# Edge loads moved to the head of two queues, the relation table's making moved behind the edge words, and the copy of the input moved behind the first pass

## The chip, the cores and the metric

The kernel runs on one core of a Trainium2 chip. A core has five engines that run their own instruction streams: TensorE (PE; its weight loads are listed as PEld), VectorE (DVE), ScalarE (ACT), GpSimd (POOL) and SyncE (SP). Transfers between the memory on the device (DRAM here) and the core's on-chip memory are DMAs. In this kernel SP and ACT issue the plain ones and POOL the indirect ones (gathers); each engine issues its DMAs in the order of its stream, and 16 DMA engines carry them out. The metric is the device time of the program in microseconds, the median of several runs.

## The reference

Four layers are applied one after the other to x (3125 nodes x 256), each with a residual: x + layer(layernorm(x)).

- A graph layer with three rounds over 103,125 directed edges (sorted by destination). Each round takes the mean of h over the incoming edges of every node, then a linear layer, a normalization with given mean and variance, and a relu.
- A mixture of 16 experts, the top 2 for each node.
- A second graph layer, in which every edge has one of 500 relation types.
- A mixture of 8 experts, the top 2 for each node.

The parts that matter here, cut down:

```python
edge_index = jnp.stack([src, dst])
x = x + _L0_gnn_ref(_layernorm(x), edge_index, ...)     # three rounds
x = x + _L0_ffn_ref(_layernorm(x)[None], ...)[0]
x = x + _L1_gnn_ref(_layernorm(x), edge_index, edge_type_500, relation_emb, ...)
x = x + _L1_ffn_ref(_layernorm(x)[None], ...)[0]

# in _L1_gnn_ref, for every edge:
gate = sigmoid(r_uv.reshape(E, -1) @ gate_w.T + gate_b)  # depends on the relation alone
m = clifford_linear(h_src * r_uv, msg_w, msg_b) * gate
```

## The kernel before, in words

Nodes are padded to 25 blocks of 128 (`NB`, `P`). The edges are laid out as 806 columns of 128 (`ET`). The kernel is written in a tile framework: the text gives operations and tiles, and the framework chooses the order in which instructions stand on each engine and places the semaphore waits. An engine runs its own stream strictly in that order, so a waiting instruction holds up everything behind it on the same engine.

**Relation table** (lines 263 to 280). The 500 relation vectors are loaded (`rel`), each is multiplied by the gate weights and summed (`prod`, `dot`), the sigmoid of the sum is the gate, and the gated vector with its gate is stored to DRAM as `r_rows`. VectorE does the products and sums, ACT the sigmoids, SP the loads and the store.

**Prologue** (391 to 470). The edge ends and types are loaded (`ids`, line 399), x into `h` (401), and on ACT's queue the weights `ww` (404, 405) and the five norm vectors (410). `first_i` (416) is the first destination of each column; from it VectorE and TensorE count where each half block of 64 destinations begins, and `begin` (433) holds 50 window starts. From the edge ends VectorE makes six words for each edge (`word`, 437 to 450), which SP stores to DRAM as `edge_words` (451). The norm vectors are folded into the weights (454 to 464), x is layer-normalized in place (466), and row 0 is replaced by the mask row (467).

**First pass** (641 to 665), which is round 1 of the first graph layer together with the sorting of the edges. For each destination block `load` reads two window starts from `begin` into registers of SP (512) and loads the two windows of 20 columns of edge words (513, `win`); `rank` begins with `kb` (523); `permute`, `lay` and `build` turn the window into a 128 x 3200 count matrix, `cell`, which is stored to DRAM as `cells` (632) for the two later rounds; `sums_of` multiplies it with the three parts of h that `spread` (339 to 353: `hT`, `part_hi`, `rest`, `part_lo`, `own`) made for each source block; `finish` writes h. `done` is the last tile that `finish` returned.

**Relation gathers** (289 to 312). The second graph layer needs `r_rows` in the order of the edge slots. All through the first pass and later stages, `fetch_relations` has POOL gather 3 x 128 rows of `r_rows` into `rel_rows` (301), and SP stores them to DRAM as `r_seq` (312) when they have landed. VectorE's operation `paced` (297) ties each group to a point of the other work. There are 4 landing buffers. `r_rows` is first read by the first gather.

**Boundary.** After the first pass a number, `loops`, tells whether a slow path must run (684). It is 0 for these inputs; the loop at 694 is skipped, but all engines meet there. Then come rounds 2 and 3 (`spread_later`, line 853, and `sums_of` with cells loaded by SP, 841). In round 2 VectorE also sums each cell over its rows (`some_src`, 863).

**Copy of x.** `base` in DRAM (320) holds a copy of the input. The third round's `finish` reads it block by block (384) for the residual. In the kernel before it is made by one DMA from DRAM to DRAM on SP (660).

Of the kernel before, what the change touches and what calls it, by code (L numbers as in the profile page):

```python
# [49 lines left out]
P = 128  # L50
# [4 lines left out]
ET = 806  # L55
D = 256
KD = D // P
NREL = 500
# [16 lines left out]
def bcast(ap, n):  # L75

    return bass.AP(tensor=ap.tensor, offset=ap.offset, ap=[[0, P], [1, n]])
# [3 lines left out]
def gnn_moe_kernel(  # L81
# [9 lines left out]
    nc = tc.nc  # L91
# [165 lines left out]
    W = D + 1  # L257
# [2 lines left out]
    of_group = [range(t, min(t + RG, NM)) for t in range(0, NM, RG)]  # L260
    r_rows = dram.tile([NREL, W], F32, name="r_rows")
    r_seq = [dram.tile([P, len(g) * W], F32, name=f"r_seq{i}") for i, g in enumerate(of_group)]
    with tc.tile_pool(name="rel_pre", bufs=1) as pre:
        gw_sb = pre.tile([P, D], F32, name="gate_w")
        nc.sync.dma_start(gw_sb, bcast(g1_gw, D))
        gb_sb = pre.tile([P, 1], F32, name="gate_b")
        nc.sync.dma_start(gb_sb, bcast(g1_gb, 1))
        NR = NREL // 4
        rel = pre.tile([NR, 4, W], F32, name="rel")
        nc.sync.dma_start(rel[:, :, :D], g1_rel.rearrange("(g p) d -> p g d", p=NR))  # L270
        for g in range(4):
            prod = pre.tile([NR, 4, 64], F32, name="prod", bufs=2)
            dot = pre.tile([NR, 1], F32, name="dot", bufs=2)
            nc.vector.tensor_mul(prod, rel[:, g, :D].rearrange("p (k c) -> p k c", k=4),
                                 gw_sb[:NR, :].rearrange("p (c k) -> p k c", k=4))
            nc.vector.tensor_reduce(dot, prod, AX.XY, ALU.add)
            nc.scalar.activation(rel[:, g, D:W], dot, AF.Sigmoid, bias=gb_sb[:NR, :])
            nc.vector.tensor_scalar(rel[:, g, :D], rel[:, g, :D], rel[:, g, D:W], None,
                                    op0=ALU.mult)
        nc.sync.dma_start(r_rows.rearrange("(g p) d -> p g d", p=NR), rel)  # L280


    next_r = iter(range(len(of_group)))
    rel_ctx = ctx.enter_context(ExitStack())
    paced = rel_ctx.enter_context(tc.tile_pool(name="paced", bufs=1)).tile([P, NM], I32, name="paced")
# [3 lines left out]
    def fetch_relations(n, after):  # L289

        for i in islice(next_r, n):
            g = of_group[i]
            rows = stage.tile([P, RG, W], F32, name="rel_rows")
            types = paced[:, g[0]:g[-1] + 1]
            nc.vector.scalar_tensor_tensor(
                types, after[:, :len(g)], 0, main_t[:, g[0]:g[-1] + 1],
                op0=ALU.bitwise_and, op1=ALU.bitwise_or)
            for j, t in enumerate(g):  # L300
                nc.gpsimd.indirect_dma_start(  # L301
                    out=rows[:, j, :], out_offset=None, in_=r_rows,
                    in_offset=bass.IndirectOffsetOnAxis(ap=types[:, j:j + 1], axis=0))
            store_relations()
            landing.append((i, rows))
# [14 lines left out]
    base = dram.tile([NP, D], F32, name="base")  # L320
    acc_d = dram.tile([NB, P, W], F32, name="acc_d")
    h = xs
    with ExitStack() as block:
# [66 lines left out]
        with ExitStack() as first:  # L390
            one = first.enter_context(tc.tile_pool(name="g0_one", bufs=1))
            begin = one.tile([1, 2 * NB], I32, name="begin")
            with ExitStack() as prep:
                pre = prep.enter_context(tc.tile_pool(name="g0_pre", bufs=1))
                psum = prep.enter_context(tc.tile_pool(name="g0_preps", bufs=2, space=PSUM))
                ids = []
                for ap in (src, dst, etype):
                    ids.append(pre.tile([P, ET], I32, name="ids", bufs=2))
                    nc.sync.dma_start(ids[-1], ap)
                for b0 in range(0, NB, 5):  # L400
                    nc.sync.dma_start(
                        h[:, b0:b0 + 5, :],
# [4 lines left out]
                for name, ap in (("b", g0_b), ("gamma", g0_gamma), ("beta", g0_beta),  # L407
# [3 lines left out]

                TF = 13
                first_i = pre.tile([ET // TF, TF], I32, name="first_i")
                nc.sync.dma_start(first_i, dst[0:1, :].rearrange("o (p k) -> (o p) k", k=TF))
                first_f = pre.tile([ET // TF, TF], F32, name="first_f")
                nc.vector.tensor_copy(first_f, first_i)
                nodes = pre.tile([ET // TF, 2 * NB, TF], F32, name="nodes")
                nc.gpsimd.iota(nodes, pattern=[[P // 2, 2 * NB], [0, TF]], base=0,  # L420
                               channel_multiplier=0, allow_small_or_imprecise_dtypes=True)
                nc.vector.tensor_tensor(
                    nodes, first_f[:, None, :].to_broadcast([ET // TF, 2 * NB, TF]), nodes,
                    op=ALU.is_lt)
# [24 lines left out]
                nc.vector.tensor_scalar(cap, cap, 1.0, None, op0=ALU.add)  # L449
                nc.vector.tensor_copy(et, ids[2])  # L450
                nc.sync.dma_start(words, word)


                nc.scalar.activation(bn["rvar"], bn["rvar"], AF.Sqrt, bias=eps)
# [6 lines left out]
                for half in range(2):  # L461
                    for k in range(KD):
# [6 lines left out]
                                                        ap=[[D, 1], [1, D]]))  # L469
# [172 lines left out]
            for i in range(NB + 3):  # L642
                if i < NB:
                    loaded[i] = load(i)
                    ranked[i] = rank(i, loaded[i])
                if 0 <= i - 1 < NB:
                    moved[i - 1] = permute(i - 1, loaded.pop(i - 1), *ranked.pop(i - 1))
                    lay(i - 1, moved[i - 1])
                    if i > 1:
                        fetch_relations(1, words_of(moved[i - 1]))  # L650
                if 0 <= i - 2 < NB:
                    if i > 2:
                        fetch_relations(1, words_of(moved[i - 2]))
                    built[i - 2] = build(i - 2, moved.pop(i - 2))
                for b in range(i * SB, min((i + 1) * SB, NB)):
                    spread(b, 0, psum.tile([P, D + 1], F32, name="z", bufs=2)[:, :D],
                           psum.tile([P, 4, P], F32, name="block", bufs=2).rearrange(
                               "p a q -> p (a q)"))
                if i == 3:
                    nc.sync.dma_start(base, x)  # L660
                if 0 <= i - 3 < NB:
                    z = sums_of(i - 3, built.pop(i - 3), 0, psum)
                    done = finish(i - 3, z, 0)
                    if i > 3:
                        fetch_relations(1, done.bitcast(I32))

        with ExitStack() as flags:
            one = flags.enter_context(tc.tile_pool(name="g0_deg0", bufs=1))
# [16 lines left out]
        with ExitStack() as slow:  # L685
# [8 lines left out]
            with tc.For_i(0, n_slow, 1):  # L694
# [4 lines left out]
                                                        ap=[[D, 1], [1, D]]))  # L699
# [10 lines left out]
                with tc.For_i(0, ET, 1) as i:  # L710
                    for e in range(2):
                        oh = []
                        for part, n in zip(ends[e], (NB, P)):
                            c = slow_work.tile([P, 1], F32, name="end_column", bufs=4)
# [3 lines left out]
                                                    op0=ALU.is_equal)  # L718
# [8 lines left out]
                for layer in range(3):  # L727
# [4 lines left out]
                    for b in range(NB):  # L732
                        mean = slow_work.tile([P, D], F32, name="mean")
                        nc.vector.tensor_scalar(mean, acc[:, b, :], inv_dst[:, b:b + 1], None,
                                                op0=ALU.mult)
# [18 lines left out]
        with ExitStack() as later:  # L754
# [104 lines left out]
            for b, cell in enumerate(ahead_of(load_cell, 2)):  # L859
                z = sums_of(b, cell, 1, psum,  # L860
                            {12: lambda: fetch_relations(1, places(b, psum))})
                d = work.tile([P, NB], F32, name="some_src")
                nc.vector.tensor_reduce(d, cell, AX.X, ALU.add)  # L863
                nc.vector.tensor_add(deg, deg, d)
                done = finish(b, z, 1)
# [25 lines left out]
            for b, cell in enumerate(ahead_of(load_cell, 2)):  # L891
# [4 lines left out]
                done = finish(b, z, 2)  # L896
# [351 lines left out]
    with ExitStack() as block:  # L1248
# [14 lines left out]
        with ExitStack() as prep:  # L1263
            pre = prep.enter_context(tc.tile_pool(name="g1_pre", bufs=1))
# [5 lines left out]
            for kern, w, name in ((km, g1_mwt, "mw"), (ku, g1_uwt, "uw")):  # L1270
# [4 lines left out]
                for bo in range(4):  # L1275
                    for bi in range(4):
                        i, sign = blades[bo][bi]
                        k, half = divmod(bi, 2)
# [262 lines left out]
```

## Time and profile before

| | us |
|---|---|
| median of 3 runs | 2874.0 (2869.36 to 2876.72) |
| the profiled execution's own time | 2875.35 |
| its span | 2873.6 |
| TensorE busy in the span | 2359.3 (82%) |
| VectorE busy | 1740.1 (61%) |
| POOL busy | 1547.9 (54%) |
| ACT busy | 420.5 (15%) |
| TensorE's first transposes of h start at | 65.06 |
| first pass, from the first `kb` to the last sums | 76.6 to 630 |
| TensorE's first transposes of round 2 start at | 640.76 |

How to read it: a row of the timeline gives the start, the length, the engine, the line, the operation with its tiles, and in brackets the idle time of the engine before it with what ended that time. An engine's name with a small q (SPq, ACTq) is its issuing side: for a DMA it is the time of the issue, not of the transfer. In the list of DMA queues, q1 holds the plain transfers issued by SP, q10 those issued by ACT, q0 the gathers of POOL. A row of the waits gives the total, the count and the longest wait. The busy time of a window says how much an engine worked in it, and not what it waited for.

### The profile page before, as it was taken

To read this page: it belongs to the slowest core of one execution; us is meant where nothing else is said; L and a number is where in the kernel's file an instruction comes from. 1 tells how busy PE (TensorE), PEld (TensorE's weight loads), DVE (VectorE), ACT (ScalarE), POOL (GpSimd) and SP (SyncE) were. 2 spreads that over 40 slices of the span, in tenths; PEclk is the share of its full clock that TensorE was granted. 3 is DMA by queue.
4 is the path that set the end of the run, shared out by engine and by line. 5 is a ranking of instruction groups with operands and counts; after the bars stand their busy time and mean duration, and the time that the engine had idled before them with its cause. 6 is when DMAs were issued, how large, how long until landed. Compare 5 with 4: busy or idle time off the path is not lost. (4 is left out here: it accounts for less than half of the span.)

```text
span 2873.6 us, 47321 instructions
## 1 busy us (share of the span) xinstructions
PE 2359.3 (82%) x17477; PEld 1907.0 (66%) x17477; DVE 1740.1 (61%) x4673; ACT 420.5 (15%) x1119; POOL 1547.9 (54%) x1349
## 2 busy tenths in 40 slices
PE   0887777768888999962998409999999997899997
PEld 0465566544777679952887407777777775688886
DVE  6988888856554567772332287888888887211111
ACT  1321222113000210000111050000000001122221
POOL 1168888870455347676555307766767662333331
PEclk9998999989998999976999759999999998899998
DMA  6147676663677559966877529878788772666664
GB/s 191 39 145 202 189 210 200 190 203 97 207 216 226 179 179 300 297 208 185 247 205 183 115 89 318 265 257 264 261 254 266 251 237 67 210 195 188 198 190 106
DMA packets 290946, 576.67 MB, mean 201 GB/s; under 512 B 77434, under 2 KB 174267, under 8 KB 286723
## 3 DMA queue, kind: packets, MB, share of 16 engines
q1 hardware_dynamic: 204243, 384.77, 39.8%
q0 software_dynamic: 73728, 173.40, 23.9%
q10 hardware_dynamic: 12720, 15.22, 1.7%
q8 instruction: 145, 2.38, 0.3%
q14 instruction: 110, 0.90, 0.1%
HBM read 430.82 MB, written 148.90 MB: 202 GB/s over the span
## 5 line engine op out<-in xcount | busy, mean ns | idle before, releaser
L301 POOL DMA_INDIRECT rel_rows<-r_rows,paced x650 | 779.5, 1199 | 567.9 <-issue 157.4
L364 PE MATMUL z<-part_hi,cell 128*128 128x256 bf16 x3750 | 679.0, 284 | 0.0
L361 PE MATMUL z<-part_lo,cell 128*128 128x256 bf16 (+1 forms) x1875 | 533.2, 284 | 7.4 <-ACT cell L631 7.2
L1470 PE MATMUL ps<-prod,d_oh 128*128 128x257 f32 x1750 | 508.3, 386 | 2.0 <-DVE prod L1461 2.0
L1458 PE MATMUL hg_ps<-hc_part,s_oh 128*128 128x257 bf16 x1950 | 325.9, 273 | 109.3 <-DVE s_oh L1414 109.3
L364 PEld LDWEIGHTS <-cell 128*128 128x128 bf16 x3750 | 375.4, 102 | 55.8 <-issue 0.8
L1201 POOL DMA_INDIRECT f_total<-y,tok_s x109 | 171.4, 1572 | 325.7 <-DVE y L1199 242.4
L250 POOL DMA_INDIRECT hg<-hc_rows,spill_s x225 | 231.4, 1029 | 211.7 <-issue 102.4
L1458 PEld LDWEIGHTS <-s_oh 128*128 128x128 bf16 x1950 | 190.3, 98 | 205.0 <-DVE s_oh L1414 109.7
L1461 DVE TENSOR_TENSOR prod<-hg_ps,rg_seq 128x257 f32<-128x257 f32 x650 | 270.0, 421 | 63.3 <-PE hg_ps L1458 58.2
L1179 PE MATMUL ph<-xT,w_t 128*128 128x256 f32 (+1 forms) x1472 | 303.3, 364 | 1.1
L1470 PEld LDWEIGHTS ps<-prod,d_oh 128*128 128x128 f32 x1750 | 275.5, 190 | 41.2 <-DVE prod L1461 23.0
L1196 PE MATMUL py<-w_t,hid 128*128 128x256 f32 x1288 | 291.0, 380 | 0.0
L1199 DVE TENSOR_SCALAR y<-py,wt_q 128x256 f32<-128x256 f32 x109 | 52.7, 484 | 392.0 <-PE py L1196 392.0
L1179 PEld LDWEIGHTS ph<-xT,w_t 128*128 128x128 f32 x1472 | 258.2, 196 | 40.0 <-DVE xT L1169 6.5
L250 POOL DMA_INDIRECT rg<-r_rows,spill_t x225 | 245.0, 1089 | 68.6 <-issue 67.3
L1196 PEld LDWEIGHTS py<-w_t,hid 128*128 128x128 f32 x1288 | 238.6, 190 | 38.4 <-DVE hid L1184 4.2
L361 PEld LDWEIGHTS <-cell 128*128 128x128 bf16 x1875 | 192.3, 103 | 35.9 <-ACT cell L631 9.3
L1188 ACT ACTIVATE hid<-ph,b_t 128x256 f32<-128x256 f32 (+1 forms) x300 | 121.8, 446 | 582.1 <-PE ph L1179 575.0
L250 POOL DMA_INDIRECT xt<-f_x,tok_g x109 | 107.4, 985 | 100.0 <-DVE wt_q L1099 40.8
L863 DVE TENSOR_REDUCE some_src<-cell 128x25 f32<-128x3200 bf16 x25 | 87.2, 3487 | 110.6 <-DMA cell<-cells 110.6
L502 DVE TENSOR_TENSOR oh_end<-held,iota 128x1024 bf16<-128x1024 f16 (+3 forms) x150 | 150.2, 1017 | 0.0
(316 smaller groups left out, 2779.9 us busy)
## 6 DMA issues: line engine op xcount, KB each, us to landing
r_seq<-rel_rows SPq DMA_DIRECT2D x216, 385.5 KB
rg_seq<-r_seq SPq DMA_DIRECT2D x216, 385.5 KB
w_t<-in_L_ffn_W_dram SPq DMA_DIRECT2D x58, 1024.0 KB
cell<-cells SPq DMA_DIRECT2D x50, 800.0 KB
w_t<-in_L_ffn_w_dram SPq DMA_DIRECT2D x68, 512.0 KB
s_row<-main_s SPq DMA_DIRECT2D x25, 832.0 KB
cells<-cell SPq DMA_DIRECT2D x25, 800.0 KB
rel_rows<-r_rows,paced POOLq DMA_INDIRECT x650
```

The lines of the kernel that those rows point to most:

```text
L250: nc.gpsimd.indirect_dma_start(out=rows, out_offset=None, in_=table, in_offset=bass.IndirectOffsetOnAxis(ap=ids, axis=0))
L301: nc.gpsimd.indirect_dma_start(out=rows[:, j, :], out_offset=None, in_=r_rows, in_offset=bass.IndirectOffsetOnAxis(ap=types[:, j:j + 1], a ...
L361: nc.tensor.matmul(z[:, :width], cell[:, sh, :], part_lo[:, sh, :width], start=sh == 0, stop=False)
L364: nc.tensor.matmul(z[:, :D], cell[:, sh, :], part_hi[:, sh, i, :], start=False, stop=sh == NB - 1 and i == 1)
L502: nc.vector.tensor_tensor(oh[:, :n, :, :], ids[:, :, None, :].to_broadcast([P, n, width, 2]), table[:, None, :width, :].to_broadcast([P, n ...
L1179: nc.tensor.matmul(ph[:, j - j0, :n], w1_t[:, 0, k, j * P:(j + 1) * P], xT[:, k, :n], start=k == 0, stop=k == KD - 1)
L1188: nc.scalar.activation(hid[:, j, :n], ph[:, j - j0, :n], act, bias=b1_t[:, j, t:t + 1])
L1196: nc.tensor.matmul(py, hid[:, j, of], w2_t[:, 0, j, :], start=False, stop=j == nj - 1)
L1201: st = nc.gpsimd.indirect_dma_start(out=total, in_=y, in_offset=None, out_offset=bass.IndirectOffsetOnAxis(ap=tok_s[:, q:q + 1], axis=0), ...
L1458: nc.tensor.matmul(hg, s_oh[:, t, :], part[:, sh, i, :W], start=i == 2, stop=i == 0)
L1461: nc.vector.tensor_mul(prod, hg, rg)
L1470: nc.tensor.matmul(ps[b], d_oh, prod, start=is_first, stop=is_last)
```

## The change

Four things move.

1. The edge loads: `src` and `etype` on SP and `dst` on ACT, with three buffers instead of two, and `first_i` on ACT right behind them in the text. In the order that the framework makes of it, ACT's stream begins with `first_i` and `dst`, SP's with `src`, `etype` and the five loads of x.
2. The making of the relation table stands behind the store of the edge words. In the framework's order SP's loads of its inputs come after those of x, its store `r_rows` after 16 of the 50 register reads of `begin`, and the mask row after 31 more.
3. The copy of x leaves the body of the first pass.
4. It stands behind the pass instead, as two DMAs: `done` (128 rows) is stored to the first rows of `base`, and the copy of x is stored over all of it. The second waits for the first, since they write the same rows.

In the first pass itself the instructions of VectorE, ACT, POOL and TensorE stand in the same order as before. At the start of round 2 the order on VectorE, ACT and TensorE differs for some hundred instructions.

```diff
-    with tc.tile_pool(name="rel_pre", bufs=1) as pre:
-        gw_sb = pre.tile([P, D], F32, name="gate_w")
-        nc.sync.dma_start(gw_sb, bcast(g1_gw, D))
...
-        nc.sync.dma_start(r_rows.rearrange("(g p) d -> p g d", p=NR), rel)
...
                 ids = []
-                for ap in (src, dst, etype):
-                    ids.append(pre.tile([P, ET], I32, name="ids", bufs=2))
-                    nc.sync.dma_start(ids[-1], ap)
+                TF = 13
+                first_i = pre.tile([ET // TF, TF], I32, name="first_i")
+                for ap, queue in ((src, nc.sync), (dst, nc.scalar), (etype, nc.sync)):
+                    ids.append(pre.tile([P, ET], I32, name="ids", bufs=3))
+                    queue.dma_start(ids[-1], ap)
+                nc.scalar.dma_start(first_i, dst[0:1, :].rearrange("o (p k) -> (o p) k", k=TF))
                 for b0 in range(0, NB, 5):
...
-                TF = 13
-                first_i = pre.tile([ET // TF, TF], I32, name="first_i")
-                nc.sync.dma_start(first_i, dst[0:1, :].rearrange("o (p k) -> (o p) k", k=TF))
                 first_f = pre.tile([ET // TF, TF], F32, name="first_f")
...
                 nc.sync.dma_start(words, word)
+
+                with tc.tile_pool(name="rel_pre", bufs=1) as rel_pre:
+                    gw_sb = rel_pre.tile([P, D], F32, name="gate_w")
+                    nc.sync.dma_start(gw_sb, bcast(g1_gw, D))
+                    gb_sb = rel_pre.tile([P, 1], F32, name="gate_b")
+                    nc.sync.dma_start(gb_sb, bcast(g1_gb, 1))
+                    NR = NREL // 4
+                    rel = rel_pre.tile([NR, 4, W], F32, name="rel")
+                    nc.sync.dma_start(rel[:, :, :D], g1_rel.rearrange("(g p) d -> p g d", p=NR))
+                    for g in range(4):
+                        prod = rel_pre.tile([NR, 4, 64], F32, name="prod", bufs=2)
+                        dot = rel_pre.tile([NR, 1], F32, name="dot", bufs=2)
+                        nc.vector.tensor_mul(prod, rel[:, g, :D].rearrange("p (k c) -> p k c", k=4),
+                                             gw_sb[:NR, :].rearrange("p (c k) -> p k c", k=4))
+                        nc.vector.tensor_reduce(dot, prod, AX.XY, ALU.add)
+                        nc.scalar.activation(rel[:, g, D:W], dot, AF.Sigmoid, bias=gb_sb[:NR, :])
+                        nc.vector.tensor_scalar(rel[:, g, :D], rel[:, g, :D], rel[:, g, D:W], None,
+                                                op0=ALU.mult)
+                    nc.sync.dma_start(r_rows.rearrange("(g p) d -> p g d", p=NR), rel)
...
-                if i == 3:
-                    nc.sync.dma_start(base, x)
                 if 0 <= i - 3 < NB:
                     z = sums_of(i - 3, built.pop(i - 3), 0, psum)
                     done = finish(i - 3, z, 0)
                     if i > 3:
                         fetch_relations(1, done.bitcast(I32))
+
+            nc.sync.dma_start(base[:P, :], done)
+            nc.sync.dma_start(base, x)
```

More of the change, by code (lines that the diff above doesn't have):

```diff
@@ L262, in gnn_moe_kernel @@
     r_seq = [dram.tile([P, len(g) * W], F32, name=f"r_seq{i}") for i, g in enumerate(of_group)]
-    with tc.tile_pool(name="rel_pre", bufs=1) as pre:
-        gw_sb = pre.tile([P, D], F32, name="gate_w")
-        nc.sync.dma_start(gw_sb, bcast(g1_gw, D))
[L266 to L279, printed above, removed]
-        nc.sync.dma_start(r_rows.rearrange("(g p) d -> p g d", p=NR), rel)
     next_r = iter(range(len(of_group)))
```

## The prediction

> **What bounds the kernel now.** I read the page, then windows of busy time cut where its stages change, then the timelines of SP, VectorE and TensorE at the places that the diff touches, then the waits of the first pass.
>
> Busy time by window (window, length, PE, PEld, DVE, ACT, POOL, granted clock, DMA share, GB/s):
>
> ```profile
> 0.00:65.00 65.00, 0.32 (x2) 0.08 (x2) 44.22 (x123) 5.00 (x8) 8.32 (x17) 1.00 0.67 212
> 65.00:77.00 12.00, 9.32 (x22) 4.31 (x23) 4.00 (x13) 3.24 (x9) 0.00 (x0) 1.00 0.14 8
> ...
> 189.00:631.00 442.00, 333.14 (x4256) 268.76 (x4255) 362.98 (x818) 92.17 (x236) 362.44 (x258) 0.91 0.67 196
> 631.00:641.00 10.00, 0.24 (x1) 0.24 (x2) 0.33 (x4) 0.00 (x0) 3.36 (x4) 0.55 0.60 190
> 641.00:668.00 27.00, 14.28 (x38) 6.84 (x37) 18.50 (x35) 4.12 (x12) 5.85 (x7) 0.66 0.96 295
> ```
>
> There are two holes in TensorE's work: the start (0 to 65) and the boundary after the first pass (631 to 641). The diff touches both. Between them stands the first pass; its waits (total us, times, longest) from 130 us on:
>
> ```profile
> DVE kb L523 <- DMA win<-edge_words: 65.7, 19, 9.7
> ...
> SPq L312 <- DMA rel_rows<-r_rows,paced: 375.9, 107, 7.6
> ...
> SPq L694 <- SPq L694: 3.9, 1, 3.9
> ```
>
> SP stands 376 us waiting for relation gathers to land, and VectorE waits for windows that SP issues late because of it. From 189 to 631 POOL makes 258 gathers; 362.4 us busy and about 0.3 us of issue between two fill the 442 us. So from 189 us the first pass runs at POOL's pace, and starting it earlier or later shifts it whole. What sets its start is the prologue, on SP and VectorE:
>
> ```profile
> 32.45 1.56 SPq L660 DMA_DIRECT2D base<-in_x_dram  x1
> 40.77 0.37 SPq L451 DMA_DIRECT2D edge_words<-word  x1
> 63.71 0.29 SPq L467 DMA_DIRECT2D xs<-in_L_gnn_mask_embed_dram  x1
> 73.16 27.20 SPq L513 DMA_DIRECT2D win<-edge_words  x6
> ...
> L512 SPq TENSOR_LOAD <-begin x50: 262/263/1195, 43.5 to 77.8; - x50
> ...
> 43.25 0.17 DVE L433 TENSOR_SCALAR begin<-begin_f 1x50 int32<-1x50 f32 x1
> ...
> 76.56 0.18 DVE L523 TENSOR_SCALAR kb<-win 128x40 f16<-128x40 f16 x1 [3.63 <-DMA win<-edge_words]
> ```
>
> The reader should see the hidden worker: SP reads the 50 window starts into registers, one by one. 31 reads stand between `begin` (43.5) and the mask row (63.71): 20.2 / 31 = 0.65 us each. Fifteen more stand before the first window (73.16): 0.61 each. TensorE's first transposes wait for the mask row (65.06, 1.35 us after its issue); `kb`, the head of the first pass, waits for the windows (76.56).
>
> The boundary:
>
> ```profile
> 629.82 4.78 SPq L312 DMA_DIRECT2D r_seq<-rel_rows  x2
> 643.63 2.83 SPq L841 DMA_DIRECT2D cell<-cells  x3
> ...
> 640.76 1.12 PE L343 MATMUL pt<-ident,xs 128*128 128x128 f32 x4 [9.80 <-SPq L694]
> ...
> 653.04 3.49 DVE L863 TENSOR_REDUCE some_src<-cell 128x25 f32<-128x3200 bf16 x1 [6.88 <-DMA cell<-cells]
> ```
>
> At the conditional loop (L694) every engine waits until SP has seen all of its DMAs land. The last is an r_seq store, issued at 634.28 and seen landed at 639.43 (5.15 us); TensorE goes on at 640.76.
>
> **The change, part by part.** All times below are on the profiled execution (2875.35 us, span 2873.6), which is 1.35 us above the median of the runs, 2874.0.
>
> *1. Loads reordered, two queues.* Ahead of the relation table now stand, on SP, src, etype and all of x; on ACT first_i, dst, the weights and the norm vectors without the sigmoids between. Everything up to the table's landing is 8.6 MB (x 3.3, weights 1.6, norm vectors 2.0, edges 1.2, table and gate 0.6). In windows without the copy the engines moved 285 (4 to 10 us), 248 (12 to 20) and 276 GB/s (22 to 29); at 0.28 that is 30 us, and packets start near 3, so the table lands at R = 33. At the 362 that the best slices show, R = 27; at 0.26, 36.
>
> A rule speaks on the second queue. The trace for 4 to 10 us:
>
> ```profile
> q10 hardware_dynamic: 1473, 1.55, 85.6%
> q1 hardware_dynamic: 308, 0.16, 16.1%
> ```
>
> The Trainium skill (DMA: Bandwidth & Descriptors, Queues, rings and completion order) says that each engine takes turns between queues. That would give SP's queue about half; the row gives ACT's queue (q10) five parts in six. By the rule the first x blocks are there by about 13 us, by the row by about 17. VectorE's order holds a statistic of x before the rest of the edge words, so `begin` follows at 18 or 22 instead of 43.25, and the edge words leave at 23 or 27 instead of 40.77. Neither decides (next step); the sum is the same by both.
>
> *2. The table made behind the words.* Its 4+4+4 VectorE instructions and 4 sigmoids cost what they did, plus one more ACT table load (1.28 us, while ACT has nothing else). But its store, `r_rows`, now stands on SP's queue behind 16 register reads and ahead of the other 34. In the changed program's order VectorE needs, from the table's landing to the store: 1.14 + 0.75 + 1.13 (products, sums), 4.95 (the reciprocal of L456, which comes between), 0.61 + 0.74 + 0.94 + 0.61 = 10.9 us. So the store issues at 33 + 10.9 = 43.9. The 16 reads are over at 27 + 10.4 = 37.4, and SP stands still for 6.5 us. Then 31 reads: 43.9 + 0.3 + 20.2 = 64.4 for the mask row (63.71 before), TensorE from 65.7. Then 3 reads: the first window at 66.3, against 73.16, landed 3.3 us later. Ahead of `kb` VectorE has two spreads, which hang on TensorE and ended at 72.94; now 73.6. So `kb` runs at 73.6 instead of 76.56: **-3.0 us**. R at 27 gives -9, R at 36 gives 0. The tail of VectorE's queue (statistics, scaling, 58 to 66 before) still ends about when it did. The first relation gather (124.64) is far behind the store.
>
> *3. The copy leaves the prologue.* Its 64 packets of 51,200 bytes took 1.9 us each, 4 per engine, ahead of edge_words. That saving is inside step 2 and worth nothing by itself, since edge_words has to be there at 66, not at 50.
>
> *4. The copy behind the first pass.* SP now does, after the r_seq store of 634.28: the store of 128 rows of `done`, the register read, then **waits for that store to land**, issues the copy, then one more r_seq store, then the loop's wait for everything. Behind it on SP: the three cell loads; at the loop's wait: all engines. The small store follows the r_seq store on its queue and shares its landing, 634.7 + 5.15 = 639.85. Copy: 1.35 us to the first packets (the mask row's trip), 4 x 1.9 = 7.6 us, 1.0 for the r_seq store behind it (128 packets of 122 ns over 16 engines): 649.9. Engines go on 1.1 us after, as before: 651.0 instead of 640.5, **+10.5 us**, with nothing beside it. The same page (Latency and other measured facts) puts a DMA's fixed cost near 2 us. With that the small store is in at 636.7 and the end at about 647.9, +7.4. I take the row, since gathers load the engines here just as they did then; ends +7 and +13.
>
> *5. The order after the boundary.* VectorE's first layer-1 work (`rest`, L350, 660.06) stood behind two reductions of cells (3.48 us each); in the changed program it stands behind four. TensorE can hold only two spreads until then. The next two reductions hold VectorE anyway in the kernel before, until 672.67, so of the 7.0 us most comes back; the fourth cell's load stands behind one relation store on SP. I take **+2**, ends 0 and +7. After that the order is nearly the same on all engines, and TensorE leads (87% busy from 668 on).
>
> Sum: -3.0 + 10.5 + 2 = +9.5. 2875.35 + 9.5 = 2884.9 for the profiled execution; 1.35 less for the median of runs: **2883.5 us**.
>
> **Rivals.**
>
> *The prologue pays more (2878).* With no gaps between the loads, the table lands at 27: -9 + 10.5 + 2 = +3.5. For it: 340 to 380 GB/s in the best slices of 4 to 10 us. Against it: SP's queue nearly alone moved 1.92 MB in the 8 us from 12 on, 240 GB/s.
>
> *The copy is hidden (2873; the other side).* One mechanism: the wait at L694 is 10 us long already, and if the small store lands at once after `done` (630.4), the copy could run inside it. It decides when the copy issues by 631: 1.35 + 7.6 + 1.0 later is 641. Then only steps 2 and 5 count, -3.0 + 2 = -1. For it: the mask row's trip of 1.35 us. Against it: SP's order has the store behind the r_seq stores, and SP waited 4.0 us there for a gather to land (630.24 to 634.24).
>
> *The boundary costs more (2891).* The copy's long packets delay the last gathers and the r_seq store, which all must land before the loop, and the fourth cell arrives late: 0 + 13 + 5 = +18 at the outer ends, +17 taken. For it: 4,112-byte gather packets share the engines at 632 to 638. Against it: SP waits for only one more group.
>
> *It doesn't do what it says.* Edges come first, but the windows still wait for 50 register reads and now for the table. That is in the forecast: 23 us earlier edges give 3 us.
>
> **How the numbers follow.** Forecast 0.52, prologue pays more 0.2, copy hidden 0.1, boundary costs more 0.18. The forecast's own range, from the ends of steps 2, 4 and 5 taken singly, is 2877 to 2889. For 8 in 10, half of each outer rival comes in: 2873 to 2893. A 0.3% change is 8.6 us, about what a measurement can tell here. Slower by more than that: 0.41 of the forecast's 0.52 (its centre is just above the bound, and the unknown ends of steps 4 and 5 lie upward) and all 0.18, with 0.02 of the first rival, 0.61. Faster: 0.05 of the hidden copy and 0.01 of the first rival, 0.06. Within: 0.33.
>
> **What the next profile would show.** Step 1: `begin` near 22 and edge_words near 27. Step 2: `r_rows` on SP near 44, in the midst of the register reads; the first window near 66, `kb` near 73.6. Step 4: no 51,200-byte packets before 50 us; 64 of them between the end of pass 1 and the first layer-1 transpose, and a gap of some 20 us there instead of 10. Step 5: four cell reductions ahead of the first `rest`. The forecast is wrong if the table lands well before 30, if the copy issues before the last r_seq store has landed, or if the first pass no longer shifts with `kb`.

## The result, and the profile after

The changed kernel took 2892.05 us (median of 8 runs, 2886.51 to 2904.46) where the kernel before took 2874.62 beside it. The medians differ by 17.4 us; the ratio estimated from all the runs is 1.0065 (95% interval 1.0046 to 1.0084), which makes 18.7 us. The forecast was +9.5, with 2877 to 2889 as its own range and 2873 to 2893 for 8 in 10. Timed again later, beside three other kernels, the change came to 1.0052 (1.0032 to 1.0071), 16.5 us by the medians.

In what follows "layer 1" is what stood above as round 2 of the first graph layer; the code counts the rounds from 0. Its "first finish" ends the first of its 25 blocks, its "last finish" the last, and "the layer-1 sums" is the stretch between the two.

The profiled execution of the changed kernel took 2894.28 us (span 2892.5). First its prologue: the timeline of SP, and then of VectorE (start, duration, engine, line, operation, out<-in, count, and in brackets the idle time before it with what ended it).

```profile
23.42 1.01 SPq L431 DMA_DIRECT2D edge_words<-word  x1
40.06 0.31 SPq L450 DMA_DIRECT2D r_rows<-rel  x1
61.07 0.28 SPq L466 DMA_DIRECT2D xs<-in_L_gnn_mask_embed_dram  x1
63.81 2.85 SPq L512 DMA_DIRECT2D win<-edge_words  x4
```

```profile
17.08 0.17 DVE L413 TENSOR_SCALAR begin<-begin_f 1x50 int32<-1x50 f32 x1
29.86 1.14 DVE L444 TENSOR_TENSOR prod<-rel,gate_w 125x256 f32<-125x256 f32 x2 [4.96 <-DMA rel<-_L_gnn_relation_emb_dram]
70.54 0.17 DVE L522 TENSOR_SCALAR kb<-win 128x40 f16<-128x40 f16 x1
```

The edge words leave SP at 23.42 instead of 40.77, but the first window is fetched only 9.35 us earlier (63.81 against 73.16): the register reads and the relation table's store at 40.06 lie between. `kb` runs at 70.54, 6.0 us earlier than before.

Then the boundary, on SP (timeline):

```profile
631.79 0.39 SPq L664 DMA_DIRECT2D base<-zt  x1
636.24 0.62 SPq L665 DMA_DIRECT2D base<-in_x_dram  x1
637.03 0.46 SPq L292 DMA_DIRECT2D r_seq<-rel_rows  x1
653.25 2.84 SPq L841 DMA_DIRECT2D cell<-cells  x3
```

SP's own waits from 130 to 660 us say why these lines stand so far apart (what waited <- for what: us in total, times, longest):

```profile
SPq L694 <- SPq L694: 11.7, 2, 10.9
...
SPq L665 <- DMA base<-zt: 2.6, 1, 2.6
```

The copy cannot be issued until the small store has landed, 4.45 us after its issue; then SP stands at the loop for 10.9 us until the copy and the relation store behind it are in. What the other engines do after that:

```profile
650.48 1.11 PE L323 MATMUL pt<-ident,xs 128*128 128x128 f32 x4 [21.74 <-SPq L694]
...
679.30 6.27 PE L326 MATMUL g<-ww,hT 128*128 128x512 f32 x8 [15.80 <-DVE own L333]
```

```profile
662.68 6.88 DVE L863 TENSOR_REDUCE some_src<-cell 128x25 f32<-128x3200 bf16 x2 [6.64 <-DMA cell<-cells]
...
670.11 3.48 DVE L863 TENSOR_REDUCE some_src<-cell 128x25 f32<-128x3200 bf16 x1
...
675.10 3.49 DVE L863 TENSOR_REDUCE some_src<-cell 128x25 f32<-128x3200 bf16 x1 [1.46 <-DMA cell<-cells]
678.50 0.41 DVE L330 TENSOR_TENSOR rest<-g,part_hi 128x256 f32<-128x256 f32 x1
```

TensorE's first layer-1 transposes start at 650.48 (640.76 before), and it then stands idle again for 15.80 us, because VectorE takes four cells' reductions ahead of the first `rest` (678.50, before 660.06). So the two kernels part like this, in us (a finish is taken at the start of the instruction that writes `zt`):

| | before | after | difference |
|---|---|---|---|
| `kb` | 76.6 | 70.5 | -6.0 |
| last finish of the first pass | 629.9 | 627.6 | -2.2 |
| first layer-1 transposes | 640.8 | 650.5 | +9.7 |
| first `rest` of layer 1 | 660.1 | 678.5 | +18.4 |
| first finish of layer 1 | 718.7 | 736.2 | +17.5 |
| last finish of layer 1 | 968.8 | 988.4 | +19.6 |
| end | 2873.6 | 2892.5 | +18.9 |

Nearly all of it is decided between 628 and 679.

### The profile page after: what moved, and what is told of

It reads as the page before. It is cut to its first block, busy times and chain, and to the rows that moved or that the text cites. A ratio compares the mean times of both kernels' runs of the same rounds, so it can differ in the third digit from the quotient of the medians.

```text
span 2892.5 us, 47319 instructions
## 1 busy us (share of the span) xinstructions
PE 2364.4 (82%) x17477; PEld 1910.1 (66%) x17477; DVE 1745.5 (60%) x4673; ACT 422.2 (15%) x1120; POOL 1546.9 (53%) x1349
```

## The experiments

Theory: three terms. The head brings a few us; the copy behind the pass lengthens the gap by some 12; and the order of the reductions after the gap costs some 8, not 2. Rivals: edges first does harm later on; the copy costs wherever it stands; the reductions have to be done anyhow, so their order is free.

**One part alone.** The first kernel puts the copy back into the pass; the second makes only that one move in the kernel before.

```diff
 # changed kernel, copy back in the pass
+                if i == 3:
+                    nc.sync.dma_start(base, x)
...
-            nc.sync.dma_start(base[:P, :], done)
-            nc.sync.dma_start(base, x)
```

> The changed kernel with the copy issued in the first pass again, where the kernel before has it (at i == 3), and no small store. Theory (boundary): all of the loss is made where the copy stands behind the first pass. Then the edges-first part alone is worth what is left at the end of the first pass: last finish near 628 (630.5 before), TensorE's first layer-1 transposes near 638, two cell reductions ahead of the first rest, and a time of 2869 to 2873 us, ratio 0.998 to 1.000. Rival (the prologue): edges first harms the later work, whose gathers now start earlier and load the engines; then the time stays above 2880 us, and the first pass ends no earlier than 630.

> The kernel before with one part of the change alone: small store and copy behind the first pass; loads, edges and relation table as before. Theory (boundary): the gap from the last finish to the first layer-1 transposes grows by 11 to 13 us and the first rest comes 6 to 9 us later still; from that +18 to +21, less whatever the prologue gains without the copy in it (0 to 3): 2890 to 2896 us, ratio 1.005 to 1.0075. Rival (the prologue): the copy costs only its own time, 7 to 8 us, and the time is 2881 to 2884 us.

Measured: the copy back in the pass gave 0.9979 (0.9963 to 0.9995; 2875.87 us, before 2879.6), the copy's move alone 1.0079 (1.0063 to 1.0094; 2900.16 us). By the ratios edges first is worth 6 us to the good, and the move of the copy costs 22.7 (by the medians 3.7 and 20.6); the sum of the ratios, +0.58%, agrees with the change's +0.65%.

With the copy back, the last finish (625.9), the first transposes (638.2) and the two reductions ahead of the first `rest` were as named; the time, 2875.87, lies above the 2869 to 2873 us named, but so did the kernel before beside it, and the ratio is at the edge of what was named. The copy's move alone cost more than named: the gap grew by 12.8 us (11 to 13 named), but the first `rest` came another 11.1 us later (6 to 9 named), and 2900.16 us lies above 2890 to 2896. Four reductions stand ahead of the first `rest` in that kernel, so it is the move of the copy that changes VectorE's order. The rival that blames the prologue is out.

**No reduction ahead of the first `rest`.** The same edit in the changed kernel and in the kernel before: each cell's reduction is tied behind that cell's finish.

```diff
-                d = work.tile([P, NB], F32, name="some_src")
-                nc.vector.tensor_reduce(d, cell, AX.X, ALU.add)
-                nc.vector.tensor_add(deg, deg, d)
                 done = finish(b, z, 1)
+                d = work.tile([P, NB], F32, name="some_src")
+                nc.vector.tensor_copy(d, done[:, :NB])
+                nc.vector.tensor_reduce(d, cell, AX.X, ALU.add)
+                nc.vector.tensor_add(deg, deg, d)
```

> The changed kernel, in which each cell's reduction (some_src) has to wait for that cell's finish, through one small copy of 128x25, so that none of them stands ahead of the first rest. Theory (order): the 18 us of reductions and cell waits ahead of the first rest are on the path; without them TensorE and VectorE go through the first spreads some 8 to 15 us sooner: first rest within 4 us of the first layer-1 transposes, time 2877 to 2884 us, ratio to the kernel before 1.001 to 1.0035. Rival (order is free): the reductions must be done anyhow and VectorE gives back what it gains, so the sums behind the spreads start no earlier: 2889 to 2895 us. Second rival (late cells): TensorE waits for the cells that SP loads late, not for VectorE; first rest comes early, but the first layer-1 sums come no earlier: 2888 to 2893 us.

> The kernel before with the same edit: each cell's reduction waits for that cell's finish. Only two reductions (13 us with the cells' wait) stand ahead of the first rest there. Theory (order): 6 to 13 us are won: 2861 to 2868 us, ratio 0.9955 to 0.998, and set beside the gain of the same edit in the changed kernel the difference is what the other two reductions cost (4 to 8 us). Rival (order is free): 2872 to 2877 us, no difference.

Measured: 0.9824 (0.9805 to 0.9844; 2828.83 us) and 0.9806 (0.9786 to 0.9825; 2820.83 us). That is 59 us off the kernel before by the second; the theory had named 6 to 13. For the changed kernel it had named 2877 to 2884 us. It was right that the front of the changed kernel would gain 8 to 15 us: the first `rest` stands 15.9 us behind the first transposes instead of 28.0 (not within 4 us, as named), and the first finish 73.5 instead of 85.7. In the kernel before, the first `rest` came 6.3 us sooner (13.0 against 19.3), but the first finish only about 1 (77.0 against 77.9). VectorE's waits from 640 to 720 us in that run show what took the place, one wait of 7.5 us for ScalarE, and ScalarE's timeline shows why: it was held at the issue of a load.

```profile
DVE part_lo L352 <- ACT part_hi L351: 10.2, 19, 7.5
```

```profile
648.35 14.74 ACTq L384 DMA_DIRECT2D xt<-base  x1
```

That load of `xt` is for the third round. What held it the profile doesn't show. So at the first finish this run doesn't test what the two reductions cost.

Most of the gain comes later, where none of the theories looked: the layer-1 sums take 197.4 and 197.5 us from first to last finish instead of 252.2 and 250.0. The waits of the kernel before from 720 to 920 us:

```profile
DVE some_src L863 <- DMA cell<-cells: 95.0, 18, 9.7
```

```profile
PE n_valid L778 <- DVE ri L786: 30.7, 9, 4.4
```

VectorE stands for 95.0 of 200 us at reductions of cells that are not yet loaded. TensorE waits behind it at the small matmuls (`n_valid`) whose inputs come from VectorE. With the reductions behind the finish neither wait is left.

**The bytes alone, and the order alone.** In the next two, only 128 of the copy's 3,200 rows stay behind the pass (3.28 MB become 0.13; waits and order stay), or only two of the four reductions are allowed ahead of the first `rest`.

```diff
 # 128 rows: small store and order as in the changed kernel
+                if i == 3:
+                    nc.sync.dma_start(base[P:, :], x[P:, :])
...
             nc.sync.dma_start(base[:P, :], done)
-            nc.sync.dma_start(base, x)
+            nc.sync.dma_start(base[:P, :], x[:P, :])
 # two ahead: the third and fourth reduction follow the second spread
                 d = work.tile([P, NB], F32, name="some_src")
+                if b in (2, 3):
+                    nc.vector.tensor_copy(d, own[:, 1, :NB])
```

> The changed kernel with only the first 128 of the copy's 3,200 rows behind the first pass, after the same small store; the other 3,072 rows are copied in the first pass where the kernel before has the whole copy. All waits and the order of work stay those of the changed kernel (four reductions ahead of the first rest); only the bytes behind the pass go down, from 3.28 MB to 0.13 MB. Theory (bytes): the gap from the last finish to the first layer-1 transposes, 22.9 us in the changed kernel and 10.9 before, falls by the 7 to 9 us for which the long packets fill the engines, to 14 to 16 us, and the time to 2882 to 2886 us, ratio to the kernel before 1.002 to 1.004. Rival (the chain): what costs is that SP stands for the small store to land and that each DMA has its own way to land; then the gap stays at 19 to 22 us and the time at 2888 to 2892 us.

> The changed kernel in which the third and the fourth cell's reduction alone have to follow the second spread (own), through one small copy of 128x25 each: two reductions ahead of the first rest, as in the kernel before; the copy stays behind the first pass. Theory (order): of the 85.7 us from the first layer-1 transposes to the first layer-1 finish, 7.8 go (77.9 in the kernel before): first rest near 671, first finish near 728, time 2883 to 2887 us, ratio to the kernel before 1.0025 to 1.004. Rival (reductions are due anyhow): VectorE does the two reductions a little later and the first finish stays near 736: 2890 to 2894 us.

Beside them stood a remedy: the copy in the layer-1 sums, where no loop waits for SP, without and with the reductions behind the finish.

```diff
             for b, cell in enumerate(ahead_of(load_cell, 2)):
...
+                if b == 2:
+                    nc.sync.dma_start(base[:P, :], done)
+                    nc.sync.dma_start(base, x)
```

> The changed kernel with small store and copy moved on, from behind the first pass to behind the third block of the layer-1 sums, where TensorE has work and no loop waits for SP. Theory (it is the place): the loop's gap is 11 us again, the order of reductions is that of the kernel before, and the copy costs 0 to 4 us for the cells and relation stores queued behind it on SP: 2869 to 2877 us, ratio 0.997 to 1.000. Rival (the copy itself costs, wherever its 3.3 MB are moved while gathers load the engines): 2882 to 2890 us.

> The last kernel, with each cell's reduction behind that cell's finish as well. From the runs so far: that edit took 61 us off the changed kernel and 56 to 59 us off the kernel before, nearly all in the layer-1 sums, where VectorE no longer stands for a cell that is not yet loaded. If the gains add up (edges first -6, copy at no cost 0 to 4, reductions late -56), 2813 to 2822 us, ratio to the kernel before 0.977 to 0.981, and it beats every kernel run. If TensorE at its full rate in the layer-1 sums is so near its bound that the rest is hidden: 2820 to 2828 us.

On that chip every kernel, the one before too (3053.93 us), was 6% longer. Ratios: 128 rows 1.0030 (1.0004 to 1.0055), two ahead 1.0063 (1.0031 to 1.0096), copy in the sums 1.0030 (1.0008 to 1.0051), that with late reductions 0.9948 (0.9923 to 0.9973). The gap with 128 rows was 11.3 us, but the intervals are too wide for the rest, and the first pass alone ended 35 to 49 us later than in the first profile of the kernel before. All four were run again on another chip.

> The kernel with 128 rows of the copy behind the first pass (the other 3,072 in the pass) once more. In its first run every kernel, the one before too, was 6% longer than on the other chips, with first-pass blocks of 21 us instead of 19.6; its gap from the last finish to the first layer-1 transposes was 11.3 us. Theory (bytes): the gap is 11 to 12 us here too, of the changed kernel's +18 us the boundary's 11 to 12 are gone, and 6 to 8 remain (four reductions ahead of the first rest, less what edges first brings): ratio to the kernel before 1.001 to 1.0035. Rival (the chain of the small store's landing): gap 19 to 22 us, ratio 1.005 to 1.0065.

> The kernel with two reductions instead of four ahead of the first rest once more (its first run: gap 20.7 us, then 84.0 us from the first layer-1 transposes to the first finish, on a chip where all was 6% longer). Theory (order): 77 to 80 us from the first layer-1 transposes to the first finish, ratio to the kernel before 1.002 to 1.004. Rival (reductions are due anyhow, the cells' landing decides): 84 to 88 us, ratio 1.005 to 1.0065.

> The kernel with the copy in the layer-1 sums once more. In its first run gap and first finish were as wanted (8.7 us, 72.9 us), but the time was 0.1 to 0.5% above the kernel before. Theory (it is the place): 0.997 to 1.000 here, as with the copy in the first pass. Rival (the copy costs where TensorE waits for cells, since SP loads them behind it): the layer-1 sums take 255 to 262 us from first to last finish instead of 250 to 252, ratio 1.001 to 1.005.

> The copy in the layer-1 sums and each cell's reduction behind its finish, once more. First run: 0.9948 to the kernel before, on the chip where gathers landed late and the layer-1 sums took 244 us from first to last finish. Theory (sums of the gains so far): with gathers in time those sums take 197 to 200 us, ratio 0.977 to 0.982. Rival (copy and cells' loads collide on SP): 205 to 215 us, ratio 0.983 to 0.988.

Measured, with the kernel before at 2873.97 us: 128 rows 1.0018 (1.0005 to 1.0032), as the theory named, with a gap of 13.7 us; that is neither the 11 to 12 of the theory nor the 19 to 22 of the rival, so the small store's chain keeps a few us of its own. Two ahead: 1.0028 (1.0013 to 1.0043), as the theory had it; but in the profile 84.1 us from the first transposes to the first finish, as the rival had it. The reason is in VectorE's order: the two reductions left the front, and other small work of the next steps moved into part of the place, so the first `rest` came 10.9 us after the first cell had landed, against 15.8 in the changed kernel and 7.0 in the one before. That edit didn't restore the old order, and it decides nothing alone. Copy in the sums: 1.0009 (0.9993 to 1.0024), with 253.6 us for the sums. It lies between theory and rival, and its interval holds both. With the late reductions: 0.9794 (0.9764 to 0.9824), as the theory named, though its sums took 206.5 us, not the theory's 197 to 200 but the rival's 205 to 215: a cell load stands on SP right behind the copy (744.91 us, the copy at 743.54), and TensorE's weight load waits 6.1 us for a cell (until 762.3).

**All terms side by side, on one chip.** The changed kernel, 128 rows, and the copy back in the pass, with the kernel before at 2871.38 us. The fourth is the candidate: edges first, copy in the pass, reductions behind the finish.

> The changed kernel itself, timed beside the next three on one chip. By its first runs (1.0065, from 1.0046 to 1.0084): 1.005 to 1.008. In the profile: 21 to 24 us from the last finish to the first layer-1 transposes, 84 to 88 us from there to the first finish.

> 128 of the 3,200 rows behind the pass, order of the reductions as in the changed kernel. Theory (three terms: bytes 9 to 11, order 8, head -3 to -6): 0.30 to 0.45% less than the changed kernel on this chip, so 1.001 to 1.0035. Rival (bytes alone make the loss, the order is free): 0.997 to 1.000, as with the copy back in the pass.

> Copy back in the pass: boundary and order as in the kernel before, only edges first is left. Theory (three terms): 0.2 to 0.4% less than the kernel with 128 rows, and 0.997 to 0.9995 to the kernel before. Rival (edges first is lost in the first pass, whose end scatters by several us from run to run): 0.9995 to 1.001.

> The last kernel with each cell's reduction behind that cell's finish. From the runs so far that edit alone gave 0.9806 and with the copy in the layer-1 sums 0.9794; with edges first at 0.9979 the product is 0.9786. Theory (the gains add): 0.976 to 0.981, the lowest time of all, 2804 to 2820 us where the kernel before takes 2874. Rival (edges first brings nothing): 0.980 to 0.982.

| kernel | median us | ratio to before (95%) | gap | first transposes to first `rest` | to first finish |
|---|---|---|---|---|---|
| before (first profile) | 2871.38 | 1 | 10.9 | 19.3 | 77.9 |
| changed | 2887.84 | 1.0052 (1.0032 to 1.0071) | 22.7 | 28.6 | 86.1 |
| 128 rows behind the pass | 2877.76 | 1.0018 (1.0005 to 1.0031) | 16.8 | 29.9 | 87.8 |
| copy back in the pass | 2866.90 | 0.9978 (0.9964 to 0.9993) | 12.0 | 19.1 | 77.4 |
| the same, reductions late | 2804.78 | 0.9748 (0.9724 to 0.9772) | 9.6 | 13.2 | 77.4 |

(The gap runs from the last finish of the first pass to the first layer-1 transposes.) Down the medians: edges first -4.5 us; the four reductions together with the small store's chain +10.9; the bytes +10.1. Each of the three can be off by some 5 us (an estimate from the intervals). The first three kernels came out as named. "The bytes alone" falls: with the bytes gone the kernel doesn't come down to that with the copy back, and the two intervals don't touch. That edges first is lost in the first pass (0.9995 to 1.001) falls too. What the order costs without the chain no pair of times separates; that split is read from the profiles. The lines behind this, first of the 128-row kernel (TensorE, VectorE), then of that with the copy back:

```profile
636.71 1.11 PE L323 MATMUL pt<-ident,xs 128*128 128x128 f32 x4 [15.69 <-SPq L696]
...
667.43 6.44 PE L326 MATMUL g<-ww,hT 128*128 128x512 f32 x8 [18.32 <-DVE own L333]
```

```profile
663.23 3.49 DVE L865 TENSOR_REDUCE some_src<-cell 128x25 f32<-128x3200 bf16 x1 [2.19 <-DMA cell<-cells]
666.63 0.41 DVE L330 TENSOR_TENSOR rest<-g,part_hi 128x256 f32<-128x256 f32 x1
```

```profile
630.47 1.12 PE L323 MATMUL pt<-ident,xs 128*128 128x128 f32 x4 [10.93 <-SPq L694]
...
650.37 5.90 PE L326 MATMUL g<-ww,hT 128*128 128x512 f32 x8 [12.50 <-DVE own L333]
```

With 128 rows TensorE's first wait is shorter (15.69 us against 21.74), while the second is longer than in the changed kernel (18.32 against 15.80): four reductions ahead, the last of them behind a cell that is 2.19 us late. So the order doesn't depend on the copy's size; with two small DMAs behind the pass four reductions still stand in front.

The candidate is 2.5% faster than the kernel before and 2.9% faster than the changed one (2804.78 us against 2887.84). Its ratio is a little below the 0.976 to 0.981 expected, although ScalarE is held at the load of `xt` here too, for 14.91 us. Its waits on VectorE and the engines' busy time from 720 to 920 us (stretch, length, then PE, PEld, DVE, ACT, POOL busy with counts, granted clock, DMA share, GB/s), followed by that stretch in the kernel before:

```profile
DVE zt L357 <- PE z L344: 49.3, 23, 3.4
```

```profile
720.00:920.00 200.00, 199.71 (x1808) 174.66 (x1806) 145.35 (x345) 5.22 (x16) 135.30 (x141) 1.00 0.90 287
```

```profile
720.00:920.00 200.00, 169.33 (x1427) 144.47 (x1425) 102.31 (x246) 0.00 (x0) 101.83 (x108) 0.90 0.69 217
```

VectorE now waits for TensorE, and TensorE for nobody.

## Why the prediction was right or wrong, point by point

**The sign** was right, and so was the main mechanism: the copy behind the pass costs more than the head brings. The size was not: +9.5 against 17 to 19.

**Step 1, loads.** `begin` was set at 18 or 22 and ran at 17.08; edge words 23 or 27, issued at 23.42; table R = 33 (27 to 36), landed by 29.86. The lower figures go with the rule of the Trainium skill (DMA: Bandwidth & Descriptors, Queues, rings and completion order), and this trace agrees with it: from 6 to 14 us the packet records show 378, 339, 346 and 331 packets of 1,024 bytes on SP's queue in each 2 us, against 339, 349, 335 and 351 on ACT's. The row of the kernel before that spoke against it (85.6% and 16.1%) was a poor measure of how two busy queues share: from 5 to 7 us of that trace SP's queue shows 107 packets, and 99 of them have 4 bytes.

**Step 2, the table's store.** The chain was right link by link, and all of it 2.5 to 4 us early with R: `r_rows` 40.06 (43.9), mask 61.07 (64.4), first window 63.81 (66.3), `kb` 70.54 (73.6). From the table's landing to its store 10.2 us passed (10.9 in the forecast). So the head brought -6.0 at `kb`, not -3.0.

**"The first pass shifts whole with `kb`"** holds for the first blocks alone: the lead is 5.8 to 7.0 us up to the sixth finish and 2.2 at the end. In three kernels with the same head and no copy in the pass, with `kb` from 71.1 to 71.7 us (copy in the sums, the same with late reductions, changed kernel again), the last finish fell at 618.4, 633.3 and 625.0. A single profile therefore can't tell how much of 6 us survives the pass. The medians can, roughly: -4.5 us and ratios of 0.9978 and 0.9979 with the copy back, whose intervals allow 1 to 11 us. That what arrives lies near the forecast's -3.0 is luck: the head gained twice as much, and the pass, which was to shift whole, gave some of it back. That the 100-odd waits of SP for relation gathers set the pass's own pace from there on is likely (379.1 us in the trace after), but no run took them away.

**Step 4, the boundary,** was nearly right: +10.5, measured +11.9 in the gap, by parts that in part cancel. The copy was issued 8.6 us after the last finish (the forecast's times make it 10.0), and TensorE went on 14.2 us after the issue (11.2), since the copy was slower: 64 packets of 51,200 bytes at mostly 2.2 to 2.5 us instead of 1.9. The small store was in 4.45 us after its issue. The row of 5.15 us was nearer than the 2 us of the Trainium skill (DMA: Bandwidth & Descriptors, Latency and other measured facts). On the chip on which all was longer, though, it took 1.85 us with two ahead (the DMA engines 21% busy meanwhile) and 2.27 with 128 rows (56%); in the other kernels that have it behind the pass 4.2 to 5.1 (47 to 74%). So the load of the engines, on which the forecast put the difference, is at most part of it. By the gaps, the bytes are worth 6 us (22.7 against 16.8, the same chip) to 9 (23.1 with two ahead against 13.7, the same chip), the chain of the small store 3 to 5.

**Step 5 is the one that failed:** +2 with ends of 0 and +7, measured about +8 to +10 in the profiles (by the medians 10.9 less the chain's 3 to 5, so 6 to 8). The first `rest` came 8.7 us later behind the first transposes (28.0 against 19.3), and the first finish 7.8 us (85.7 against 77.9); with 128 rows against the copy back it was 10.4 (87.8 against 77.4). In the first pair of profiles step 5 makes 5.8 of the 9.4 us that the forecast is short; 0.8 come from the head, 1.4 from step 4, and 1.4 arise later. The forecast counted the four reductions rightly and then took it that "of the 7.0 us most comes back", since VectorE does the third and the fourth in either kernel. It took VectorE for the engine that sets this stretch. In the kernel before, the third and the fourth reduction stand behind the first `rest`:

```profile
660.06 0.41 DVE L350 TENSOR_TENSOR rest<-g,part_hi 128x256 f32<-128x256 f32 x1
...
662.30 3.48 DVE L863 TENSOR_REDUCE some_src<-cell 128x25 f32<-128x3200 bf16 x1
...
669.28 3.48 DVE L863 TENSOR_REDUCE some_src<-cell 128x25 f32<-128x3200 bf16 x1
```

The stretch from the first `rest` to the first finish, before and after, shows which engine sets it:

```profile
660.06:718.70 58.64, 57.77 (x214) 30.13 (x215) 39.48 (x100) 24.36 (x69) 0.00 (x0) 0.95 0.15 40
```

```profile
678.50:736.20 57.70, 56.90 (x207) 29.55 (x208) 34.77 (x97) 24.34 (x69) 0.00 (x0) 0.95 0.00 1
```

TensorE (the first busy figure) is busy for 57.77 of 58.64 us and 56.90 of 57.70. VectorE has 39.48 and 34.77 us of work in it. Before, reductions three and four lay inside this stretch beside TensorE's work and cost next to nothing. Moved in front of it, they lie where TensorE has two spreads and then nothing, and every us of them counts; taking them away from behind TensorE's work gave only 0.9 us back (58.64 against 57.70). The wait for the fourth cell (1.46 us, 2.19 with 128 rows) comes on top.

**The rivals.** "The boundary costs more" (2891) gave nearly the measured time, in part by luck: the gap was +11.9, not +13, and the head brought something; the fourth cell did come late as it said, by 1.46 us, but most of what it lacked was the two reductions. "The copy is hidden" fell: the copy was issued at 636.24, and it would have had to be 631. "The prologue pays more" was right on its row (-6.0 lies between -3 and -9) and was outweighed. "It doesn't do what it says" holds in part: edge words 17.4 us sooner became 6.0 at `kb`. (Its "23 us earlier edges" doesn't fit its own step 1, by which the edge words leave 14 to 18 us sooner.) The three terms -4.5, +10.9 and +10.1 add up to the changed kernel's +16.5 us by the way they were taken, so that is no check; the independent one is the first pair of experiments, +0.58% against +0.65%.

## What to carry to other kernels

When work moves from one side of a wait to the other, ask of each stretch which engine fills it: work of another engine is free inside the stretch and costs its whole length in front of it. A transfer put just before a point at which all engines wait for all DMAs has no cover, neither for its bytes nor for the landing of what it is ordered behind. And an engine that reads a tile as soon as it might be there blocks its own queue for whatever else stands in it: here a side sum that nobody needed soon, moved behind the finish, gave more than the whole change was about.

## What was not expected of the hardware

- With the waits gone from the layer-1 sums, the granted clock in that stretch was 1.00 instead of 0.90, at 287 instead of 217 GB/s on the DMA engines: the busier TensorE was given the higher clock. A matmul of `z` took 273 ns in the mean instead of 288. How much of the 52 to 55 us is clock was not separated.
- While TensorE stood still at the boundary, its granted clock was 0.50 (631 to 650 us of the trace after), and 0.69 in the 18 us behind it.
- The copy's 51,200-byte packets took mostly 2.2 to 2.5 us (2.0 to 2.8 in all) with nothing else on the engines until 646.9 us, when all of them had started, longer than the 1.9 us in the prologue of the kernel before. The place is not the reason: with edges first and the copy back in the pass they took 2.3 us too, from 31 to 42 us.
- Why the copy in the layer-1 sums stays at 1.0009 where the copy in the pass gives 0.9978 is not settled. Its profile points to SP's queue: the cell loads on either side of the copy are issued 21.4 us apart (722.70 and 744.08), and one reduction waits 19.2 us for its cell, where the longest such wait before was 9.7. Why a pass with the same head ends up to 15 us apart is open.
